# A mixture-of-experts layer stack: first rows loaded first, routed gathers further ahead, more routed weights held

## The chip, the cores and the metric

The kernel runs on one core of a Trainium2 chip. The metric is the device time of one execution in microseconds (us), the median of several runs; less is better. All data is float32.

The engines are named as the profile names them: PE (matrix multiply; PEld is its weight load), DVE (vector), ACT (scalar functions), POOL (here it issues the indirect DMAs: gathers of rows by an index, and adds of rows into memory by an index), and SP (it issues all other DMAs and computes nothing). Each engine takes its instructions in the order in which they were written and waits at each until its semaphores say that it may start.

## The reference, cut to what matters

The input x has 8 sequences of 512 tokens by 256 channels. Four layers follow each other.

```python
# 1 adapter, weights chosen by a language id per sequence
h = relu(x @ W1[id] + b1[id]);  c0 = layernorm(x + h @ W2[id] + b2[id]) * gamma[id] + beta[id]
# 2 experts choose tokens: 8 experts, each takes its 128 best tokens of every sequence
Sm = softmax(c0 @ Wg.T);  G, I = top_k(Sm transposed, 128)
x1 = x;  x1[b, I] += G * (gelu(c0[b, I] @ W1[e] + b1[e]) @ W2[e] + b2[e])
# 3 conditioning: scans over time, gates, a projection and a layernorm  -> c1
# 4 tokens choose experts: 64 experts, 8 per token, at most 128 tokens per expert
w, ids = top_k(softmax(c1 @ router.T), 8);  w = w / sum(w)
y_e = (silu(rows_e @ w_gate[e]) * (rows_e @ w_up[e])) @ w_down[e]
out = x1 + sum over e of w * y_e  +  (silu(c1 @ s_gate) * (c1 @ s_up)) @ s_down
```

The residuals around the layers are kept in memory (x1 in `x1_rows`, the sum in `out` and a second array `odd`).

## The kernel before

**How the order is made.** The kernel is written as steps: each has an engine, an estimated cost, the keys that it reads and writes, the buffers (rings) that it takes, a rank, and optionally `after`, other steps that must have been placed first. `Order.run` plays these steps against a simple clock and calls their functions in the order in which it lets them start; that is the order of instructions on each engine. Its clock knows one DMA rate (0.19 MB per us) and takes, among steps that can start within 0.25 us, the one of lowest rank. The numbers in it thus change the order of instructions and nothing else. What an instruction waits for on the chip follows from the tiles that it reads and writes, and from the reuse of DMA semaphores.

**Start.** `warm` lets PE multiply the identity seven times four times. `adapter(b)` loads the transposed rows of sequence b (`axb`, `load_xb`), its plain rows (`axt`, `load_xt`), and by POOL gathers the two adapter matrices (`row_w1`, `row_w2`). `down` multiplies on PE (L372), `relu` is on ACT, `up` on PE (L392; for sequences 2 to 4 it also adds axt by a multiplication with the identity, L396), the sum and the statistics are on DVE (L401, L423) for sequences 0, 1 and 5 to 7, and on ACT for 2 to 4. `norm` (ACT, L473), a transposition (PE, L266) with a copy by ACT (L281), and `scores` (PE, L489) follow. Sequences 0 and 1 are the first group: `choose(0)` takes their 128 best tokens per expert in 16 rounds on DVE (L523 to L561), and its lists are turned on PE at L574. `choose(1)` does the same for the other six. `w_load` loads the small weights of the later layers; `hb` is half of the biases that it brings in `cb`.

**Experts.** `expert(n)` runs 32 units (4 pairs of sequences by 8 experts): weights `fw1`, `fw2`, gathers `xg` (L629), PE L642, L663, L730, and adds into `x1_rows`. Behind each pair's experts, `conditioning(b)` and `route(g)` run beside the next pair's. The last pair has none beside it: there DVE ranks tokens (L1229) until `last_lists` writes the 64 lists `ix_c1`. The lower half of the last ranking goes to other partitions by a 32 KB DMA, `rsecond` (L1261), and is merged at L1248.

**Routed experts.** Weights come in 32 pairs of 1.18 MB each (`wpair`, L1398), 6 in the ring `wfar`, 6 in the ring `wnear`. The first six are loaded during the tail of the experts, the next six behind sequence 7's conditioning, ahead of `rsecond`, and pair p beyond that into the place of pair p - 12. `routed(e)` has a gather of 128 rows `xe` (POOL, L1421, a ring of 6), transposition and copy, `gate_up` (PE, L1440), `silu`, `mul`, a transposition (L1455), `down` (PE, L1463 and L1464), a copy `xye` (DVE, L1467), and an `add` into memory (POOL, L1470): even experts into `out`, odd ones into `odd`. Two adds into one array follow each other: the second waits until the first has landed. In the order on POOL eight gathers go ahead of the first add, and later one to three gathers stand between two adds into the same array.

**End.** `total(b)` loads odd and out, adds them and stores the sum.

Of the kernel before, what the change touches and what calls it, by code (L numbers as in the profile page):

```python
# [17 lines left out]
P = 128  # L18
# [7 lines left out]
NH = H // P  # L26
PAIR = 2 * 2 * (H // P) * F1 + 3 * H
FAR = 6
NEAR = 6
WARM = 7  # L30
LATE = ()
EPS = 1e-5
NEG = -3.0e38
# [112 lines left out]
def kernel(ctx: ExitStack, tc: tile.TileContext, d: dict, out: bass.AP):  # L146
# [65 lines left out]

        "rlr": 2, "rtk": 1, "rm8": 2, "rev": 1, "rhalf": 1, "rsecond": 1, "rws": 1, "rc1b": 2, "rsl": 1, "rob": 1,

        "wfar": FAR, "wnear": NEAR, "xe": 6, "xhe": 4, "xeT": 3, "xsl": 2, "xheT": 2, "xye": 4, "xob": len(LATE),
    }
    WHERE = {"mm": "ps", "hid": "ps", "res": "ps"}
    WHERE.update({k: "pa" for k in RINGS if k.startswith("a")})
# [32 lines left out]
    def load(size, fn, **k):  # L251
        return order.add("SP", 0.1, fn, size=size, **k)
# [60 lines left out]
    def adapter(b):  # L313
# [39 lines left out]
            t = tile_of(hT, "ahT", [A + 1, S])  # L353
            nc.gpsimd.memset(t[A : A + 1, :], 1.0)

        rows = []
        if b == 0:
            load(512 * KB, load_xb, new=[(xb, "axb")], rank=b)
        rows.append(pool(1.1, row_w1, new=[(w1, "aw1")], rank=rank - 3, lag=2.5))
        rows.append(pool(1.1, row_w2, new=[(w2, "aw2")], rank=rank - 3, lag=2.5))  # L360

        if b:
            load(512 * KB, load_xb, new=[(xb, "axb")], rank=b, after=rows[:1] if b == 1 else first_up)
        load(512 * KB, load_xt, new=[(xt, "axt")], rank=b, after=rows[1:] if early_one else first_up)
        pool(1.0, one, new=[(hT, "ahT")], rank=rank)
        pool(1.1, row_gains, w=[("gains", b)], rank=rank + 2, lag=2.5)

# [7 lines left out]
            nc.scalar.activation(V[hT][:A, :], V["ph", b][:A, :], AF.Relu, bias=V[w2][:A, H : H + 1])  # L375

        s = pe(2.0 * hot, down, r=[w1, xb, w2, hT], new=[(("ph", b), "mm")], rank=rank, after=() if early_one else begun)
        if early_one:
            first_up[:] = [s]
        act(0.7, relu, r=[("ph", b), w2], w=[hT], rank=rank)  # L380

        sums = ("asum", b)
        for g in range(NC // 2):
# [29 lines left out]
                dve(0.75, add, r=[po, xt], w=[xa], rank=rank)  # L413
            else:
                act(1.1, add, r=[po], w=[xa, sums], rank=rank)
        load(512 * KB, keep, r=[xt], w=[("x1", b)], rank=rank + 5)

        mv, sd = ("amv", b), ("asd", b)
        if by_dve:
# [59 lines left out]
            nc.sync.dma_start(out=c0_rows[b].rearrange("(c p) h -> p c h", p=P), in_=V[c0])  # L479

        act(2.4, norm, r=[xa, ("anm", b)], new=[(c0, "ac0")], rank=rank)
        load(512 * KB, store, r=[c0], w=[("c0", b)], rank=rank)
        turned(c0, c0T, "ac0T", None, rank, lambda: gains[:, b, :], [("gains", b)])

        def scores():
# [26 lines left out]
    def choose(g):  # L512
        n = len(groups[g])
        rank = 10 if g == 0 else 60
        lg = lgs[g]
        lgr = lg.rearrange("p q h (b e) -> p (q h b) e", e=E0)
        G, R = NC * n, n * E0
        K = ("choice", g)
        t = {}

        def less():
            t["mx"] = only([P, G], F32, name=f"mx{g}")
            nc.vector.tensor_reduce(t["mx"], lgr, AX.X, ALU.max)  # L523
            nc.vector.tensor_tensor(lgr, lgr, t["mx"].unsqueeze(2).to_broadcast([P, G, E0]), ALU.subtract)

        def exp():
            nc.scalar.activation(lgr, lgr, AF.Exp)

        def share():
            t["sm"] = only([P, G], F32, name=f"sm{g}")  # L530
            nc.vector.tensor_reduce(t["sm"], lgr, AX.X, ALU.add)
            nc.vector.reciprocal(t["sm"], t["sm"])
            nc.vector.tensor_tensor(lgr, lgr, t["sm"].unsqueeze(2).to_broadcast([P, G, E0]), ALU.mult)

        def turn():
            pt = bank(("cpt", g))
            for q in range(NC // 2):
                nc.tensor.transpose(
                    pt[: 2 * R, q * P : (q + 1) * P], lg[:, q].rearrange("p h r -> p (h r)"), ident
                )  # L540

        def keep():
            t["prob"] = only([2 * R, S // 2], F32, name=f"prob{g}")
            t["best"] = only([2 * R, K0], F32, name=f"best{g}")
            t["best_i"] = only([2 * R, K0], U32, name=f"best_i{g}")
            nc.vector.tensor_copy(t["prob"], V["cpt", g][: 2 * R, : S // 2])

        dve(0.8, less, r=[("lg", g, b) for b in groups[g]], w=[K], rank=rank)
        act(0.35, exp, w=[K], rank=rank, table="e")
        dve(0.9, share, w=[K], rank=rank)  # L550
        pe(0.7, turn, r=[K], new=[(("cpt", g), "mm")], rank=rank)
        s = dve(0.5, keep, r=[("cpt", g)], w=[K], rank=rank)
        if g == 0:
            begun.append(s)
        for i in range(K0 // 8):
            def one(i=i):
                prob, best, best_i = (t[k] for k in ("prob", "best", "best_i"))
                o = slice(8 * i, 8 * i + 8)
                nc.vector.max(best[:, o], prob)
                nc.vector.max_index(best_i[:, o], best[:, o], prob)  # L560
                nc.vector.match_replace(prob, best[:, o], prob, -1.0)  # L561

            dve(1.6, one, w=[K], rank=rank)


        def lists_of():
            t["lists"] = [only([2 * R, K0], F32, name=f"best{k}{g}") for k in "fbr"]
            for dst, src in zip(t["lists"], (t["best_i"], t["best_i"][:, ::-1], t["best"][:, ::-1])):
                nc.vector.tensor_copy(dst, src)

        def turn_lists():
            pt = bank(("clt", g))
            for k, src in enumerate((*t["lists"], t["best"])):
                nc.tensor.transpose(pt[:, 2 * R * k : 2 * R * (k + 1)], src, ident[: 2 * R, : 2 * R])  # L574

        def keep_lists():
            gT = r0.tile([P, R], F32, name=f"gT{g}")
            ix = r0.tile([P, R], I32, name=f"ix{g}")
            first_ones = only([P, R], F32, name=f"fo{g}")
            apart = only([P, R], F32, name=f"ap{g}")  # L580
            n1, n2, v2, v1 = (V["clt", g][:, R * k : R * (k + 1)] for k in (0, 3, 5, 6))
            held = only([P, 2, R], F32, name=f"hd{g}")
            nc.vector.tensor_copy(held[:, 0], n1)
            nc.vector.tensor_copy(held[:, 1], v1)
            nc.vector.tensor_tensor(first_ones, held[:, 1], v2, ALU.is_ge)
            nc.vector.tensor_tensor(gT, held[:, 1], v2, ALU.max)
            half = float(S // 2)
            nc.vector.scalar_tensor_tensor(apart, n2, half, held[:, 0], ALU.add, ALU.subtract)
            nc.vector.tensor_tensor(apart, apart, first_ones, ALU.mult)
            nc.vector.scalar_tensor_tensor(ix, n2, half, apart, ALU.add, ALU.subtract)  # L590
            for b in groups[g]:
                o = (b - groups[g][0]) * E0
                lists[b] = ix[:, o : o + E0], gT[:, o : o + E0]

        dve(0.9, lists_of, w=[K], rank=rank)
        pe(0.5, turn_lists, r=[K], new=[(("clt", g), "mm")], rank=rank)
        dve(1.6, keep_lists, r=[("clt", g)], w=[("lists", g)], rank=rank)
# [4 lines left out]
    def expert(n):  # L602
# [16 lines left out]
        def load_3():  # L619
            nc.sync.dma_start(out=tile_of(b2, "fb2", [P, H]), in_=d["fb2"][e : e + 1, :].to_broadcast([P, H]))  # L620

        load(1024 * KB, load_1, new=[(w1, "fw1")], rank=20 + n, after=first_up)
        load(1024 * KB, load_2, new=[(w2, "fw2")], rank=20 + n, after=first_up)
        load(128 * KB, load_3, new=[(b2, "fb2")], rank=20 + n, after=first_up)

        which = 0 if bs[0] in groups[0] else 1
# [133 lines left out]
    def one(name, shape, src, size, rank=30):  # L760
        def fn():
            W[name] = wp.tile(shape, F32, name=name)
            nc.sync.dma_start(out=W[name], in_=src)
        load(size, fn, w=[name], rank=rank)

    def w_load():

# [623 lines left out]
    def pair(p):  # L1391

        q = p - FAR
        ring = "wfar" if q < 0 or q % (FAR + NEAR) >= NEAR else "wnear"

        def fetch():
            t = tile_of(("pair", p), ring, [P, PAIR])
            nc.sync.dma_start(out=t, in_=d["wpair"][p])  # L1398

        load(PAIR * P * 3, fetch, new=[(("pair", p), ring)], rank=400 + 2 * p, after=last_expert if p < FAR else last_tokens)  # L1400

    def hidden_places():

        def fill():
            for k in range(4):
                t = V["he", k] = tile_of(("he", k), "xhe", [P, 2 * P])
                nc.gpsimd.memset(t[:, F1:] if k % 2 == 0 else t[:, : 2 * P - F1], 0.0)

        pool(1.0, fill, w=[("he", k) for k in range(4)], rank=399, after=last_tokens)

    def routed(e):
        rank = 400 + e
# [60 lines left out]
            )  # L1473

        rows = [(k, b) for b in range(B) for k in ("rows", "shares")]
        pool(1.3, gather, r=["slots", *rows], new=[(xe, "xe")], rank=rank, lag=3.0)
        pe(0.35, turn_x, r=[xe], new=[(px, "mm"), (xeT, "xeT")], rank=rank)
        act(0.9, scale, r=[px, "lgb"], w=[xeT], rank=rank)
        pe(1.3, gate_up, r=[xeT, wp_], new=[(pgu, "hid"), (sl, "xsl")], rank=rank)
# [1 line left out]
        dve(0.5, mul, r=[pgu, sl, xe], w=[he], rank=rank)  # L1481
        pe(0.3, turn_h, r=[he], new=[(pt, "mm"), (heT, "xheT")], rank=rank)
        dve(0.45, keep, r=[pt], w=[heT], rank=rank)
        pe(0.9, down, r=[heT, wp_], new=[(po, "res"), (ye, "xye")], rank=rank)
        dve(0.45, out_of, r=[po], w=[ye], rank=rank)
        pool(1.9, add, r=[ye, *(("sum", j, b) for b in range(B))], w=[("chain", j)], rank=rank, lag=3.0)

# [56 lines left out]
    last_lists()  # L1544
    for b in range(B):
        shared(b)
    for p in range(E1 // 2):
        pair(p)
    hidden_places()
    for e in range(E1):  # L1550
        routed(e)
    for b in range(B):
        total(b)
# [76 lines left out]
```

## Time and profile before

| what | value |
|---|---|
| median of 3 runs | 1177.99 us (1172.96 to 1183.5) |
| profiled execution | 1173.81 us, of it span 1172.0 us |
| PE busy, mean granted clock | 1029.4 us (88%), 0.949 |
| DVE, ACT, POOL busy | 685.1, 486.6, 379.7 us |
| DMA | 221.74 MB, mean 189 GB/s |
| start until expert 0's rows are turned (L642) | 0 to 80.1 us |
| experts and conditioning | 80 to 899 us |
| routed experts (first gather to last add) | 899.4 to 1133.8 us |
| end | to 1172 us |

The span runs from the first to the last instruction that the profiler saw on the core; the execution's own time is 1.8 us longer. A busy share is an average over these stages, which have different limits, so the stages are read one by one, and an idle engine matters only where the next work waits for it.

### The profile page before, as it was taken

What the parts mean: (1) busy time and instruction counts of PE and PEld (TensorE: products, weight loads), DVE (VectorE), ACT (ScalarE), POOL (GpSimd) and SP (SyncE); (2) the same over time, 40 slices, a digit from 0 to 9 for tenths busy, and PEclk for the clock granted to TensorE, in tenths of its full rate; (3) what the DMA queues carried; (4) which work ended last, traced back from release to release, by engine and by line L of the source; (5) the groups of instructions that cost most, each with busy time, mean ns of one, the idle gap of its engine ahead of it and who ended that gap; (6) DMA issues with size and microseconds to landing.
All of it is one profiled execution on the core that took longest, in us unless ns stands there. A gap on an engine that the chain in (4) does not pass through costs nothing. (4 is left out here: it accounts for less than half of the span.)

```text
span 1172.0 us, 12980 instructions
## 1 busy us (share of the span) xinstructions
PE 1029.4 (88%) x4317; PEld 758.2 (65%) x4317; DVE 685.1 (58%) x1447; ACT 486.6 (42%) x1012; POOL 379.7 (32%) x305
## 2 busy tenths in 40 slices
PE   7889999999989999989999999999886888678850
PEld 5668888867778776878686877445453555446530
DVE  3543630169983788965798947698766332233323
ACT  2567444443546444536444535423342333223310
POOL 7231333313232213333222212000002676657850
PEclk8779999999999999999999999999997999899985
DMA  8954666767356775456763634932146888795568
GB/s 263 352 166 151 190 191 197 238 204 217 102 169 202 221 239 162 143 145 208 244 209 112 175 93 120 372 108 71 60 162 227 232 241 237 200 270 93 91 132 355
DMA packets 89602, 221.74 MB, mean 189 GB/s; under 512 B 14896, under 2 KB 62488, under 8 KB 77120
## 3 DMA queue, kind: packets, MB, share of 16 engines
q1 hardware_dynamic: 63936, 183.91, 45.0%
q0 software_dynamic: 25600, 37.01, 16.6%
q8 instruction: 34, 0.56, 0.2%
q14 instruction: 32, 0.26, 0.1%
HBM read 177.69 MB, written 47.32 MB: 192 GB/s over the span
## 5 line engine op out<-in xcount | busy, mean ns | idle before, releaser
L663 PE MATMUL hid<-exT,fw 128*128 128x256 f32 x1024 | 231.6, 382 | 3.3 <-ACT hf L673 3.3
L730 PE MATMUL res<-fw,hf 128*128 128x256 f32 x1024 | 233.0, 379 | 0.0
L663 PEld LDWEIGHTS hid<-exT,fw 128*128 128x128 f32 x1024 | 193.8, 191 | 31.7 <-ACT hf L673 4.5
L730 PEld LDWEIGHTS res<-fw,hf 128*128 128x128 f32 x1024 | 191.6, 190 | 25.7 <-issue 1.4
L748 POOL DMA_INDIRECT x_rows<-y,ix x64 | 117.2, 1832 | 235.9 <-ACT y L745 225.2
L629 POOL DMA_INDIRECT xg<-c_rows,ix x64 | 65.8, 1029 | 241.6 <-PE hid L642 201.8
L673 ACT ACTIVATE hf<-hid,fb 128x256 f32<-128x256 f32 x256 | 104.6, 472 | 76.1 <-PE hid L663 76.0
L1005 DVE TENSOR_TENSOR_SCAN t<-alpha,u 128x512 f32<-128x512 f32 x84 | 102.8, 1224 | 2.9
L994 DVE SCALAR_TENSOR_TENSOR u<-gx,blend,mdb 128x512 f32<-128x512 f32 x128 | 95.3, 745 | 1.1
L745 ACT ACTIVATE y<-y,gT 128x256 f32<-128x256 f32 x64 | 32.2, 507 | 143.5 <-DVE y L742 143.5
L1467 DVE COPY xye<-res 128x256 f32<-128x256 f32 x64 | 27.1, 424 | 106.6 <-PE res L1464 97.3
L1421 POOL DMA_INDIRECT xe<-c_rows,ix_c x64 | 63.6, 993 | 55.4 <-DVE ix_c L1308 35.6
L281 ACT ACTIVATE xeT<-mm,lgb 128x128 f32<-128x128 f32 x128 | 50.4, 455 | 48.6 <-PE mm L1430 46.7
L742 DVE TENSOR_TENSOR y<-res,fb 128x256 f32<-128x256 f32 x64 | 26.6, 419 | 73.4 <-PE res L730 73.3
L1443 ACT ACTIVATE xsl<-hid 128x192 f32<-128x192 f32 x64 | 21.2, 331 | 104.3 <-PE hid L1440 104.3
L281 ACT ACTIVATE exT<-hid,gains 128x128 f32<-128x128 f32 x128 | 48.1, 457 | 29.3 <-PE hid L642 29.3
L1007 DVE TENSOR_TENSOR tmp<-tmp,t 128x512 f32<-128x512 f32 x84 | 58.1, 692 | 2.9
L1470 POOL DMA_INDIRECT out_dram<-xye,ix_c x32 | 51.0, 1592 | 25.7 <-DVE xhe L1446 7.6
L1470 POOL DMA_INDIRECT odd<-xye,ix_c x32 | 50.9, 1590 | 23.4 <-issue 8.0
L1440 PE MATMUL hid<-wfar,xeT 128*128 128x384 f32 x144 | 54.7, 505 | 0.0
L1430 PE MATMUL mm<-ident,xe 128*128 128x128 f32 x128 | 25.3, 292 | 32.7 <-DMA xe<-c_rows,ix_c 32.4
L1458 DVE COPY xheT<-mm 128x256 f32<-128x256 f32 x64 | 26.9, 421 | 45.4 <-PE mm L1455 45.4
(210 smaller groups left out, 1613.1 us busy)
## 6 DMA issues: line engine op xcount, KB each, us to landing
fw<-in_fw_dram SPq DMA_DIRECT2D x64, 1024.0 KB
wfar<-in_wpair_dram SPq DMA_DIRECT2D x18, 1152.0 KB
mdb<-md_rows SPq DMA_DIRECT2D x32, 512.0 KB
wnear<-in_wpair_dram SPq DMA_DIRECT2D x14, 1152.0 KB
axb<-in_xT_dram SPq DMA_DIRECT2D x8, 512.0 KB
axt<-in_x_dram SPq DMA_DIRECT2D x8, 512.0 KB
x_rows<-axt SPq DMA_DIRECT2D x8, 512.0 KB
fb<-in_fb_dram SPq DMA_DIRECT2D x32, 128.0 KB
```

Of the source, the lines that this page charges most:

```text
L281: nc.scalar.activation(dst, src, AF.Identity, bias=gain[:, NH + hc : NH + hc + 1], scale=gain[:, hc : hc + 1])
L629: nc.gpsimd.indirect_dma_start(out=tile_of(("xg", u, b), "xg", [P, H]), out_offset=None, in_=c0_rows[b], in_offset=bass.IndirectOffsetOnAx ...
L663: nc.tensor.matmul(t[:, i, :], V[w1][:, hc, f * P : (f + 1) * P], V[exT][:, hc, :], start=hc == 0, stop=hc == NH - 1,)
L673: nc.scalar.activation(t[:, i, :], p[:, i, :], AF.Gelu_apprx_tanh, bias=fb1[:, e, f : f + 1])
L730: nc.tensor.matmul(V[res][:, :H], V[hf][:, i, j * K0 : (j + 1) * K0], V[w2][:, f, :], start=f == 0, stop=f == NF - 1,)
L748: nc.gpsimd.indirect_dma_start(out=x1_rows[b], out_offset=bass.IndirectOffsetOnAxis(ap=lists[b][0][:, e : e + 1], axis=0), in_=V[y], in_of ...
L994: nc.vector.scalar_tensor_tensor(u, V[K["gx"]][:, hc, :], W["blend"][:, hc, k : k + 1], V[mdb][:, k % 2, :], ALU.mult, ALU.mult,)
L1005: nc.vector.tensor_tensor_scan(t, decay(1 + k), u, 0.0, ALU.mult, ALU.add)
L1007: nc.vector.tensor_tensor(whole, whole, t, ALU.add)
L1421: nc.gpsimd.indirect_dma_start(out=tile_of(xe, "xe", [P, H + E1]), out_offset=None, in_=c1_rows, in_offset=bass.IndirectOffsetOnAxis(ap=ix ...
L1440: nc.tensor.matmul(t[:, : 2 * F1], V[xeT][:, hc, :], wgu()[:, hc, :], start=hc == 0, stop=hc == NH - 1)
L1470: nc.gpsimd.indirect_dma_start(out=odd if j else out, out_offset=bass.IndirectOffsetOnAxis(ap=ix_c1[:, e : e + 1], axis=0), in_=V[ye], in_ ...
```

## The change

It does five things. The two loads of the first sequences' rows (axb and axt of 0, then of 1) are issued ahead of all weights, and the small weights of later layers come behind the first experts' weights. A group of warm-up multiplications is left out (`WARM` 6). The ring of gathered rows has 8 places, and gathers have a rank five experts ahead of the adds. `wnear` has 8 places, so 14 pairs are held. A load of a pair beyond these is given `after` the down step of expert 3n + 1 (n counts from the first such pair). Besides, several estimates that the planner uses are changed: sizes of some loads are halved, one round of the choice costs 1.65 for 1.6, the lag of a gather 5 for 3.

```diff
-NEAR = 6
-WARM = 7
+NEAR = 8
+PACE = 30
+WARM = 6
...
-        "wfar": FAR, "wnear": NEAR, "xe": 6, "xhe": 4, "xeT": 3, "xsl": 2, "xheT": 2, "xye": 4, "xob": len(LATE),
+        "wfar": FAR, "wnear": NEAR, "xe": 8, "xhe": 4, "xeT": 3, "xsl": 2, "xheT": 2, "xye": 4, "xob": len(LATE),
...
-        rows = []
-        if b == 0:
-            load(512 * KB, load_xb, new=[(xb, "axb")], rank=b)
-        rows.append(pool(1.1, row_w1, new=[(w1, "aw1")], rank=rank - 3, lag=2.5))
-        rows.append(pool(1.1, row_w2, new=[(w2, "aw2")], rank=rank - 3, lag=2.5))
-
-        if b:
-            load(512 * KB, load_xb, new=[(xb, "axb")], rank=b, after=rows[:1] if b == 1 else first_up)
-        load(512 * KB, load_xt, new=[(xt, "axt")], rank=b, after=rows[1:] if early_one else first_up)
+        pool(1.1, row_w1, new=[(w1, "aw1")], rank=rank - 3, lag=2.5)
+        pool(1.1, row_w2, new=[(w2, "aw2")], rank=rank - 3, lag=2.5)
+        load(256 * KB, load_xb, new=[(xb, "axb")], rank=b, after=() if early_one else first_up)
+        load(256 * KB, load_xt, new=[(xt, "axt")], rank=b + 0.2, after=() if early_one else first_up)
...
-        if early_one:
-            first_up[:] = [s]
+        if b == 0:
+            first_up.append(s)
...
-            dve(1.6, one, w=[K], rank=rank)
+            dve(1.65, one, w=[K], rank=rank)
...
-        load(1024 * KB, load_1, new=[(w1, "fw1")], rank=20 + n, after=first_up)
-        load(1024 * KB, load_2, new=[(w2, "fw2")], rank=20 + n, after=first_up)
+        early_part = 0.5 if n < 2 else 1
+        load(1024 * KB * early_part, load_1, new=[(w1, "fw1")], rank=20 + n, after=first_up)
+        load(1024 * KB * early_part, load_2, new=[(w2, "fw2")], rank=20 + n, after=first_up)
...
-        load(size, fn, w=[name], rank=rank)
+        load(size / 2, fn, w=[name], rank=rank, after=() if rank < 0 else first_up)
...
-        load(PAIR * P * 3, fetch, new=[(("pair", p), ring)], rank=400 + 2 * p, after=last_expert if p < FAR else last_tokens)
+
+        n = p - FAR - NEAR
+        after = last_expert if p < FAR else last_tokens if n < 0 else downs[PACE * n // 10 + 1 :][:1]
+        load(PAIR * P * 3, fetch, new=[(("pair", p), ring)], rank=400 + 2 * p, after=after)
...
-        pool(1.3, gather, r=["slots", *rows], new=[(xe, "xe")], rank=rank, lag=3.0)
+        pool(1.3, gather, r=["slots", *rows], new=[(xe, "xe")], rank=rank - 5, lag=5.0)
...
-        pe(0.9, down, r=[heT, wp_], new=[(po, "res"), (ye, "xye")], rank=rank)
+        downs.append(pe(0.9, down, r=[heT, wp_], new=[(po, "res"), (ye, "xye")], rank=rank))
...
-    for p in range(E1 // 2):
-        pair(p)
     hidden_places()
     for e in range(E1):
+        if e % 2 == 0:
+            pair(e // 2)
         routed(e)
```

In the order that this builds, PE has both early downs ahead of both early ups, and all adapter steps up to sequence 7's up ahead of expert 0's first transposition; before, expert 0 stood among them. DVE takes hb between the copies of the two score tiles. POOL issues ten gathers ahead of the first add, and from the thirteenth expert on one gather and one add in turn. SP has eight pairs ahead of rsecond, then 18 pairs in a row. Between expert 2 and the last gathering of tokens the orders differ in nothing that matters here.

## Prediction

> **What bounds the kernel now.** I read first the table of windows, cut where the kernel changes stage (columns: window, its length, busy time and instructions of PE, PEld, DVE, ACT, POOL, granted clock, DMA share, GB/s).
>
> ```profile
> 10.00:40.00 30.00, 21.37 (x80) 15.23 (x78) 8.17 (x28) 10.47 (x18) 13.18 (x16) 0.69 1.00 359
> 40.00:80.00 40.00, 32.94 (x122) 23.06 (x123) 25.49 (x102) 22.99 (x72) 12.11 (x14) 0.77 0.73 253
> 80.00:150.00 70.00, 68.91 (x362) 59.98 (x361) 35.43 (x122) 43.88 (x89) 20.84 (x18) 0.98 0.54 168
> 872.00:899.00 27.00, 14.18 (x40) 8.16 (x39) 25.05 (x67) 3.53 (x6) 0.00 (x0) 0.80 0.75 289
> 899.00:1053.00 154.00, 122.56 (x494) 82.81 (x494) 45.95 (x122) 46.22 (x124) 101.54 (x80) 0.93 0.83 231
> 1053.00:1134.00 81.00, 67.69 (x282) 45.46 (x282) 27.44 (x73) 25.88 (x69) 63.88 (x48) 0.96 0.54 92
> ```
>
> From 80 to 700 us PE is full (68.91 of 70 us in the third row) and the change moves no instruction there, so a microsecond won before it reaches the end. Before 80 us PE idles 15.7 us of 70 and runs at 0.69 and 0.77 of its clock: a chain of waits sets the pace. From 899 to 1134 PE isn't full either. There POOL is: the page gives 993 ns for a gather (L1421) and 1591 ns for an add (L1470), and nearly every POOL row follows the last by 0.30 us. One expert costs POOL 0.99 + 0.30 + 1.59 + 0.30 = 3.18 us, so 48 instructions in the last row are 63.9 + 48 x 0.30 = 78.3 of 81 us. With weights loading, 80 instructions are 101.5 + 24.0 = 125.5 of 154: 28.5 us stalled. The timeline of POOL shows such a stall:
>
> ```profile
> 1004.14 1.62 POOL L1470 DMA_INDIRECT odd<-xye,ix_c  x1 [0.30 <-DVE xhe L1446]
> 1006.06 0.99 POOL L1421 DMA_INDIRECT xe<-c_rows,ix_c  x1 [0.30 <-issue]
> 1007.35 1.60 POOL L1470 DMA_INDIRECT out_dram<-xye,ix_c  x1 [0.30 <-issue]
> 1011.37 1.58 POOL L1470 DMA_INDIRECT odd<-xye,ix_c  x1 [2.42 <-issue]
> ```
>
> The add at 1011.37 found its data long ready; it waited for the earlier add into the same array, odd, to land. How long an add takes to land is in the view of L1470, with weights loading and then without:
>
> ```profile
> DMA to landing us min/median/max: 3.7/5.6/10.2
> ...
> DMA to landing us min/median/max: 3.6/3.8/4.7
> ```
>
> **Part 1, the start.** The timeline, cut to the links of the chain:
>
> ```profile
> 11.15 0.47 SPq L327 DMA_DIRECT2D axt<-in_x_dram  x1
> ...
> 19.36 1.29 DVE L401 TENSOR_TENSOR axa<-mm,axt 128x512 f32<-128x512 f32 x2 [11.78 <-DMA axt<-in_x_dram]
> ...
> 20.74 3.75 PE L372 MATMUL mm<-axb,aw 128*128 128x512 f32 x4 [5.44 <-DMA gains<-in_cgb_dram,ix_w]
> ...
> 30.91 2.08 ACT L473 ACTIVATE ac<-axa,anm,ars 128x256 f32<-128x256 f32 x4 [0.44 <-DVE anm L436]
> ...
> 39.41 0.22 DVE L523 TENSOR_REDUCE mx<-lg 128x8 f32<-128x64 f32 x1
> ...
> 67.52 0.28 PE L574 MATMUL mm<-ident,bestf 32*128 32x32 f32 x1 [3.87 <-DVE bestb L569]
> ```
>
> Sequence 0's axt is issued behind fifteen other loads (2.1 MB) and lands at 19.3; sequence 1's down (20.74) follows; the two scores are chosen at 39.41 and the lists turned at 67.52. Afterwards SP issues axb, axt of both sequences within about 4.5 us, 2.1 MB, landed by about 11.5 at the 0.30 MB/us that moved here.
>
> They don't then start at 11.5, for here **a rule speaks against the change**. The Trainium skill (DMA: Bandwidth & Descriptors, "Issuing engines are not separate DMA queues") says that transfers of all issuing engines interleave on the same 16 DMA engines: POOL's four row gathers, which the matmuls need as much, are not hurried by moving SP's loads. The trace agrees: the second took 3.2 us to land, the third, issued at 7.45 into heavier SP traffic, 6.3 us (13.7), the fourth 6.6 us (15.3). If the x loads alone decided, down 1 could start near 11.5 and the gain would be 6 us; by the gathers it starts at 13.8. I take the row.
>
> Then, with before's durations: down 1 ends at 15.7 (1.88), up 0, now ordered behind it, 17.7 (1.96), up 1 19.7. DVE: add 0 to 18.5, its statistics 2.2 to 20.6, add 1 and two small steps to 22.3, statistics 1 24.4. ACT: norm 0 to 23.8, the turned copy 1.6 to 26.1, root and scale, so norm 1 at 26.9 against 30.91: **4.0 us**. The links to 67.52 stay the same length: lists turned at 63.5. On the way PE now also does one more down (1.9) and an up with its identity matmuls (3.5) that before came after 67.5: 5.4 us of PE work in what was idle time. Together 9.4. But the changed PE order puts all adapters ahead of expert 0, so no expert matmul fills the gaps while ACT norms and copies: from norm 2 (about 56) ACT needs some 39 us (six norms at 2.1, six copies at 1.6, sequence 4's sums and squares 4.5, the rest 12) until the last copy at 95. PE's own work from the lists to the last score is 42.7 us before (67.5 to 110.2), less 9.6 that now lies earlier or later, so 96.6: the two are close enough to collide. I take off 1.4: **-8 us**; between +1 (gaps eat all) and -13 (no gap, gathers on time).
>
> Other weights now load behind the first expert weights. Only hb on DVE needs one early (cb): 9.2 MB ahead of it at 0.36 MB/us put it near 31, DVE asks at about 34; if cover fails it costs the difference. One warm-up group less saves 1.35 us of PE in front of a gather: 0. New planner costs and sizes cost nothing themselves; what they reorder is counted above.
>
> **Part 2, two more pairs before the routed stage.**
>
> ```profile
> 871.56 2.99 SPq L1398 DMA_DIRECT2D wnear<-in_wpair_dram  x6
> ...
> 894.57 0.49 SPq L1261 DMA_DIRECT2D rsecond<-rhalf  x1
> ...
> 897.61 0.28 DVE L1248 TENSOR_TENSOR list<-list,rsecond 64x128 f32<-64x128 f32 x1
> ...
> 899.42 1.02 POOL L1421 DMA_INDIRECT xe<-c_rows,ix_c  x1 [35.62 <-DVE ix_c L1308]
> ```
>
> The six loads (7.08 MB) run at 0.43 MB/us until 891, then the store to odd, and the queue is empty at 894.57, when rsecond's 32 KB go; the last merge has them by 897.61. Eight loads last 2.36/0.43 = 5.5 us longer, the queue to about 897.2.[...] The row of axt, issued at 11.15 and landed at 19.3 behind 2 MB, says that transfers of one queue wait their turn: rsecond lands near 899.4. I take the row: **+1.8 us** (0 to 4), on everything after it, POOL's first gather included. Two loads fewer in the routed stage pay in part 3.
>
> **Part 3, the routed stage.** The number of POOL instructions stays, so its floor stays: 64 x 3.18 = 203.5 us against 234.4 now (899.4 to 1133.8), 31 us of stall. What changes is the order. Between two adds into the same array stood one, two or three gathers: 5.07, 6.36 or 7.65 us. Afterwards, past a head of ten gathers, always two: 6.36. An add follows the landing by 0.73 us, so landings up to 5.6 us are then free; with one gather only up to 4.3. Laying before's own 64 landing times along both orders gives stalls of 29.6 us (before) and 27.0: the long landings, 8 to 10 us, stall in either. That PE waits 32.4 us for gathers (L1430) is no gain: where POOL is full they can't come sooner.
>
> **The pace isn't there.** `after=downs[...]` only tells the planner when it may write a load down. In the built SP order nothing stands between the routed loads, and each waits only for PE to be done with the pair fourteen earlier and for the eighth DMA before it. So loads still go at one for two experts, as now, where pairs wait for their place:
>
> ```profile
> SPq L1398 <- PE res L1464: 90.8, 14, 12.4
> ```
>
> They end with expert 35 instead of 39; those four stalled little in excess: another -0.3. Sum of part 3: **-3 us**, bounded by +6 (landings half a microsecond longer: 18 us per microsecond, as below) and -27 (no stall).
>
> **Sum.** -8 + 1.8 - 3 = -9.2 us on the profiled execution's own 1173.8 us (span 1172.0): 1164.6. The median shown, 1178.0, lies 4.2 above it and would give 1168.8; I take the middle, 1167.
>
> **Rivals.**
> - *Start swallowed* (0.24): the ACT-paced adapters keep PE waiting and expert 0 is turned at 80, as now. For it: ACT's 39 us. Against: PE saves a real 5.4 us of work. Part 1 is then 0: 1175.
> - *Stalls go* (0.10): steady gathers even out DMA bursts and landings fall under 5.6 us everywhere: -27 for -3, 1143. For it: 3.8 us without loads. Against: one load per two experts as before, 1.18 MB each.
> - *Slower* (0.09): adds land later. Each microsecond of mean landing beyond 5.6 costs half a microsecond for each of 36 loaded experts, 18 us; at 7.0 instead of the measured 5.65 +24: 1191. It outweighs the start from 6.2 on. For it: DMA share already 0.83, tighter gathers. Against: total bytes are unchanged.
> - *Main case* 0.57: 1167, own range 1157 to 1176.
>
> About 1% is what a measurement of this kernel can tell from no change. Faster by over 1% (under 1166): half of the main case, stalls go, a little of the first rival: 0.45. Slower: the third and a stray: 0.10. Same: 0.45. The range 1147 to 1182 leaves out most of the slower case and of the end of the second.
>
> **What would show it.** axa's wait for axt gone; the choice's first reduction at 34 to 37 instead of 39.4; lists turned at 62 to 65; rsecond's merge later against rhalf by 1 to 3 us; waits of L1398's successor still one per two experts, last load after expert 35; landings unchanged in the loaded stretch. Wrong if expert 0 starts no sooner relative to the lists' turn and PE is idle from 65 to 95, or if the routed stage moves by over 8 us.

## The result, and the profile after

The changed kernel takes 1172.3 us (median of 20 runs, 1165.13 to 1180.27) where the kernel before takes 1179.72 (20 runs): ratio **0.9933**, 95% interval 0.9909 to 0.9956, by which it is 7.9 us less (the medians differ by 7.4). Measured once more beside the experiments it was 0.9946 (0.9922 to 0.9970).

The two profiled executions don't show that difference: 1174.22 us after, 1173.81 before. The 20 executions of one kernel lie 13 to 15 us apart, and the first profile of before was among its shortest; a second one, taken later, has 1178.66. So in what follows the times decide how much a kernel gains, and the profiles where. The profiled execution of `g_only` was one of its slow ones, over 1.5% longer than its fastest, and no stage of it is read.

The table of windows of the changed kernel, cut as that of before (columns as there):

```profile
10.00:40.00 30.00, 23.08 (x77) 16.25 (x78) 10.30 (x39) 10.65 (x18) 13.15 (x16) 0.66 0.94 324
40.00:80.00 40.00, 34.22 (x124) 25.40 (x123) 24.24 (x96) 25.15 (x75) 12.04 (x14) 0.76 0.89 304
80.00:150.00 70.00, 69.53 (x344) 57.93 (x344) 39.12 (x141) 37.92 (x79) 19.22 (x17) 0.92 0.43 129
872.00:899.00 27.00, 19.61 (x49) 10.70 (x47) 24.67 (x55) 6.78 (x10) 0.00 (x0) 0.84 0.89 351
899.00:1053.00 154.00, 119.84 (x483) 81.41 (x484) 49.02 (x139) 45.54 (x122) 99.44 (x79) 0.92 0.81 225
1053.00:1134.00 81.00, 67.91 (x296) 46.67 (x294) 29.03 (x76) 27.25 (x72) 64.49 (x49) 1.00 0.53 87
```

The third row is the surprise: PE is as full as before from 80 to 150, but its granted clock is 0.92 instead of 0.98, and 344 of its instructions fit in instead of 362. The timeline has the links of the start. Both downs now run one behind the other from 11.69 on, when the gathered matrix of the first has landed:

```profile
11.69 5.40 PE L368 MATMUL mm<-axb,aw 128*128 128x512 f32 x8 [2.43 <-DMA aw<-in_cw_dram,ix_w]
...
27.49 2.07 ACT L469 ACTIVATE ac<-axa,anm,ars 128x256 f32<-128x256 f32 x4 [0.44 <-DVE anm L432]
...
36.15 0.22 DVE L519 TENSOR_REDUCE mx<-lg 128x8 f32<-128x64 f32 x1
...
66.32 0.21 DVE L565 CAST bestb<-best_i 32x128 f32<-32x128 uint32 x1
...
70.75 0.25 PE L570 MATMUL mm<-ident,bestf 32*128 32x32 f32 x1
```

Norm 1 is 3.4 us earlier than before and the choice 3.3. But the choice ends only 1.0 us earlier (the same cast of the last result is at 67.30 before), and the lists are turned 3.2 us *later*. ACT shows the first loss. Before (sequence 2's root, L458, and its norm; then the end of the choice on DVE):

```profile
54.84 0.30 ACT L458 ACTIVATE asd<-asq,eps 128x4 f32<-128x4 f32 x1
...
56.32 2.07 ACT L473 ACTIVATE ac<-axa,anm,ars 128x256 f32<-128x256 f32 x4
...
67.30 0.21 DVE L569 CAST bestb<-best_i 32x128 f32<-32x128 uint32 x1
```

After (root and norm are the fourth and fifth line, behind them what waits for them on DVE and PE):

```profile
54.91 0.67 ACT L371 ACTIVATE ahT<-mm,aw 64x512 f32<-64x512 f32 x1
57.48 0.68 ACT L371 ACTIVATE ahT<-mm,aw 64x512 f32<-64x512 f32 x1 [1.91 <-DMA aw<-in_cw_dram,ix_w]
58.19 1.28 ACT L454 ACT_TABLE_LOAD   x1
59.48 0.48 ACT L454 ACTIVATE asd<-asq,eps 128x4 f32<-128x4 f32 x2
60.22 4.04 ACT L469 ACTIVATE ac<-axa,anm,ars 128x256 f32<-128x256 f32 x8 [0.26 <-DVE anm L459]
...
59.81 0.18 DVE L458 RECIPROCAL ars<-asd 128x4 f32<-128x4 f32 x1 [3.22 <-ACT asd L454]
...
60.87 2.80 PE L267 MATMUL mm<-ident,ac 128*128 128x128 f32 x8 [4.46 <-ACT ac L469]
```

Sequence 2's squares were done at 51.2, but its root now stands behind sequence 3's squares and two relus, of which one waits 1.91 us for a gathered matrix. Two things hang on it: DVE, in the middle of the choice, waits 3.22 us for the root (1.23 before), and PE is idle for 4.46 us until the norm lets it turn sequence 2. Then the lists, ready at 66.5, wait on PE behind sequence 4's up and sequence 2's scores:

```profile
68.54 0.59 PE L392 MATMUL mm<-axt,ident 128*128 128x256 f32 x2
68.97 1.85 PE L485 MATMUL mm<-fwg,ac0T 128*128 128x8 f32 x16
```

In the routed stage the pace of the loads and the landings are what they were. First the waits of SP (us in total, times, longest: 6.7 us each, one for two experts), then the landings of L1472 with weights loading and without:

```profile
SPq L1395 <- PE res L1466: 86.7, 13, 10.3
```

```profile
DMA to landing us min/median/max: 3.7/5.5/9.0
DMA to landing us min/median/max: 3.6/3.8/3.9
```

The last load goes at 1043.8, beside the end of expert 35 (its result copied at 1044.2). The stage takes 228.7 us (907.0 to 1135.7) instead of 234.3, and rsecond's merge comes 4.9 us behind its issue instead of 3.0.

### The profile page after: what moved, and what is told of

Read it like the earlier page. It is cut to its first block, busy times and chain, and to the rows that moved or that the text cites. A ratio compares the mean times of both kernels' runs of the same rounds, so it can differ in the third digit from the quotient of the medians.

```text
span 1172.3 us, 12994 instructions
## 1 busy us (share of the span) xinstructions
PE 1035.4 (88%) x4309; PEld 763.3 (65%) x4309; DVE 685.1 (58%) x1447; ACT 484.5 (41%) x1010; POOL 380.2 (32%) x305
## 4 chain that ended last, share of the span: by engine, by line
PE 42%; DVE 32%; DMA 14%; issue 6%; POOL 3%; ACT 2%; SPq 0%; POOLq 0%; DVEq 0%; ACTq 0%
PE res L727 10%; PE hid L660 9%; DVE t L1002 9%; DVE u L991 7%; DVE tmp L1004 4%; DMA odd<-xye,ix_c 4%; PE mm L931 3%; DVE tr L1002 3%; DMA out_dram<-xye,ix_c 3%; PE mm L1039 2%; DMA xe<-c_rows,ix_c 2%; PE hid L1442 2%; PE mm L267 2%; DMA rc1b<-c1T_rows 2%; POOL xe L1423 2%
## 5 line engine op out<-in xcount | busy, mean ns | idle before, releaser
L1472 POOL DMA_INDIRECT out_dram<-xye,ix_c x32 | 50.5, 1580 | 22.6 <-DVE xheT L1460 7.5
L1472 POOL DMA_INDIRECT odd<-xye,ix_c x32 | 50.5, 1578 | 21.4 <-DVE xye L1469 9.3
L1442 PE MATMUL hid<-wnear,xeT 128*128 128x384 f32 x128 | 48.8, 505 | 0.0
L1442 PE MATMUL hid<-wfar,xeT 128*128 128x384 f32 x128 | 47.4, 495 | 0.0
```

The source lines that it names most:

```text
L1442: nc.tensor.matmul(t[:, : 2 * F1], V[xeT][:, hc, :], wgu()[:, hc, :], start=hc == 0, stop=hc == NH - 1)
L1472: nc.gpsimd.indirect_dma_start(out=odd if j else out, out_offset=bass.IndirectOffsetOnAxis(ap=ix_c1[:, e : e + 1], axis=0), in_=V[ye], in_ ...
```

## The experiments

All twelve kernels, stage by stage. "Unit 2" is the start of the third expert's multiplications (L663 before), by when both orders have done the same work but for the warm-up group; the routed stage runs from the first gather to the end of the last add.

| kernel | ratio to before (95%) | unit 2 | unit 2 to rsecond | issue to merge | routed |
|---|---|---|---|---|---|
| before, twice | 1 | 130.8, 130.9 | 763.8, 767.1 | 3.0, 3.0 | 234.3, 237.0 |
| after, twice | 0.9933 (0.9909-0.9956), 0.9946 (0.9922-0.9970) | 134.3, 129.7 | 766.0, 769.3 | 4.9, 4.2 | 228.7, 230.7 |
| s_only | 0.9978 (0.9954-1.0002) | 127.2 | 767.3 | 3.0 | 240.7 |
| g_only | 0.9952 (0.9931-0.9973) | | | | |
| n_only | 1.0008 (0.9980-1.0036) | 131.3 | 770.7 | 4.9 | 232.0 |
| sg | 0.9942 (0.9922-0.9963) | 132.7 | 766.1 | 3.0 | 237.1 |
| root_first | 0.9949 (0.9927-0.9971) | 129.2 | 768.4 | 4.6 | 232.6 |
| act_q | 0.9945 (0.9920-0.9971) | 134.9 | 763.1 | 5.6 | 229.3 |
| pace | 0.9969 (0.9947-0.9992) | 124.1 | 769.4 | 5.6 | 235.1 |
| mixed | 0.9947 (0.9917-0.9978) | 126.5 | 766.3 | 4.7 | 229.9 |
| best | 0.9911 (0.9880-0.9941) | 130.3 | 764.9 | 3.0 | 235.2 |
| four | (part left out) | 132.3 | 763.5 | 5.7 | 208.9 |

### The parts alone

**s_only**: before with every hunk of the start, and WARM 6.

> The kernel before with the start alone changed (first rows' loads ahead, small weights behind the first expert weights, six warm-up groups, the start's planner costs). The forecast's step (-8 us) expects 0.993 of before, the lists turned near 63 and expert unit 2 some 6 to 8 us earlier than the 130.8 of before. The profile of the changed kernel says otherwise: choice begun at 36.2 instead of 39.4, lists turned at 70.8 instead of 67.5, unit 2 at 134.3. If that profile is typical, this kernel shows unit 2 3 to 4 us later than before and a ratio of 1.002 to 1.004.

Ratio 0.9978: 2.6 us gained, between 5.4 gained and 0.2 lost. Unit 2 came at 127.2, not at 134: neither of the two expectations, the gain of 6 to 8 us least of all. Its choice and lists have the times of the changed kernel (35.6, 70.6), so what differs between 127 and 134 lies after the lists.

**g_only**: before with

```diff
-"xe": 6,
+"xe": 8,
-pool(1.3, gather, ..., rank=rank, lag=3.0)
+pool(1.3, gather, ..., rank=rank - 5, lag=5.0)
```

> The kernel before with the gathers alone changed (8 places for gathered rows, rank five ahead, lag 5). The forecast: stalls of POOL in the loaded stretch from 28.5 to about 26 us, 0.998 of before. The rival 'stalls go': 0.977. If the changed kernel's profile (routed stage 228.7 us against 234.4) is typical and the gathers cause it: 0.995. The start has before's order: unit 2 at 130.8 and rsecond's merge at 897.6 within what differs from run to run, which this run measures.

0.9952: 5.7 us gained (3.2 to 8.1). That is more than forecast, near the 0.995 that the changed kernel's profile had suggested, and far from "stalls go".

**n_only**: before with

```diff
-NEAR = 6
+NEAR = 8
```

> The kernel before with eight places in wnear alone, so 14 pairs held and no other load paced differently. The forecast: rsecond's merge 1.8 us later against rhalf's end and next to nothing back, 1.001 of before. By the changed kernel's profile (merge 4.7 us later after its start is taken off): merge near 902, ratio 1.003, unless the last loads, now three pairs earlier relative to the experts, save stalls at the end of the loaded stretch.

1.0008: nothing, within 0.28%. The profile shows both sides of it. The merge waits 4.9 us instead of 3.0, and the routed stage is shorter (232.0; 234.3 to 240.7 in the three profiles with the same gathers and twelve pairs). The profiled execution is again one of the shorter ones (1179.2; median 1182.9). The three parts multiply to 0.9978 x 0.9952 x 1.0008 = 0.9938: they add up.

**after_again**: the changed kernel.

> The changed kernel once more, for a second profile and more times. Its twenty times gave 0.9933 of before, yet its profiled execution (1174.2) is no shorter than that of before (1173.8). If the first profile was typical: choice at 36, lists turned at 70.8, unit 2 at 134.3, first routed gather at 907. If the draw of one execution decides: unit 2 near 125 to 128 and the first gather some 5 to 8 us earlier. Ratio 0.991 to 0.996 under either.

Unit 2 came at 129.7 and the first gather at 905.0, between the two expectations, with the lists turned at 70.4, much as in the first profile. So the two differ in what lies between the lists and unit 2.

**before_again**: the kernel before.

> The kernel before, for a second profile. The first was among the shortest of its executions (1173.8, median of all 1180). Stage by stage, if that draw was short in the routed stage: 238 to 241 us there instead of 234.3 (240.7 in the kernel with the start alone changed, whose routed stage is the same). If it was short in the start: unit 2 at 134 or more with a clock below 1.0 between 75 and 95.

Unit 2 came at 130.9 again, the clock as in the first profile; the 4.9 us between the two executions lie 3.3 behind unit 2 and ahead of rsecond and 2.7 in the routed stage (237.0, a little under the expected 238 to 241), less 1.3 at the end. Before and after, each as the mean of its two profiles: start +1.1, middle +2.2, merge +1.5, routed stage 235.7 to 229.7, **-6.0**, end -1.1. In all that is 2.2 us less, not 7.9: the middle, where the orders differ in nothing that matters, and the start scatter by as much as is to be explained. But what the profiles show as gained, they show in the routed stage.

**sg**: start and gathers, wnear at 6.

> Start and gathers changed, wnear left at 6 places. If the parts add up (0.9978 x 0.9952): 0.993, as fast as the whole change, and the two more pairs are worth nothing. If the two more pairs help the new order of gathers (the routed stage took 228.7 and 230.7 us in the changed kernel's two profiles, 241.5 with the gathers alone): 0.995 or more here, with POOL stalled 28 us and not 22, and with rsecond's merge 3.0 us behind its issue, not 4.2 to 4.9.

0.9942 (0.9922 to 0.9963) holds the sum of its parts, 0.9930, and is no slower than the whole change: by time the two more pairs are worth nothing. The profile has the routed stage at 237.1 instead of 229 to 231, with the merge back at 3.0 us. But this execution is one of the longest of its 22 (1179.0; median 1173.3), by about as much as its stage is longer, so that by itself it doesn't show what the missing pairs cost.

### Where the start's gain went

**root_first**: the changed kernel with

```diff
-act(0.35, root_of, r=[("asq", b)], ...)
+roots.append(act(0.35, root_of, r=[("asq", b)], ...))
-act(1.1, add, r=[po], w=[xa, sums], rank=rank)
+act(1.1, add, r=[po], w=[xa, sums], rank=rank, after=roots[:1] if b == 3 else ())
```

> The changed kernel, with sequence 3's first sum on ACT held back until sequence 2's root, so that ACT takes that root before sequence 3's squares and before the relu that waits for gathered matrices. Theory: what the start didn't gain was lost at this root, 59.5 in the changed kernel against 54.8 before. Then norm 2 starts near 54 instead of 60.2, the choice's wait for the root falls from 3.2 to about 1 us, PE's 4.5 us idle ahead of it go, and expert unit 2 comes about 4 us earlier than in the changed kernel at the same clock (127 and less): 0.9965 of the changed kernel, 0.990 of before. Rival: PE, throttled after its early idle stretches, sets the pace whatever ACT does; then unit 2 stays at 127 to 134 and the ratio at 0.994.

The chain did as the theory says; from its timelines of ACT and PE:

```profile
50.43 0.30 ACT L456 ACTIVATE asd<-asq,eps 128x4 f32<-128x4 f32 x1
...
51.34 2.06 ACT L471 ACTIVATE ac<-axa,anm,ars 128x256 f32<-128x256 f32 x4
...
64.68 0.24 PE L572 MATMUL mm<-ident,bestf 32*128 32x32 f32 x1
```

Norm 2 is 8.9 us earlier than in the changed kernel and the lists 6.1. And yet the ratio stays at 0.9949 and unit 2 at 129.2, as the rival in the expectation had it. The edit did more than was meant: the planner now also put expert 0's first transposition ahead of the last adapters, where PE waits for its rows (0.67 us here, 1.47 for the next one):

```profile
72.82 0.33 PE L641 MATMUL hid<-ident,xg 128*128 128x128 f32 x1 [0.67 <-DMA xg<-c_rows,ix]
```

Most of the rest is in the windows (clock: third column from the right). Before:

```profile
70.00:80.00 10.00, 9.95 (x45) 7.20 (x44) 0.48 (x3) 6.19 (x22) 5.76 (x7) 0.88 0.85 277
80.00:90.00 10.00, 10.00 (x51) 8.06 (x50) 3.72 (x12) 8.68 (x20) 5.28 (x6) 1.00 0.37 114
```

The changed kernel:

```profile
70.00:80.00 10.00, 10.00 (x45) 9.20 (x45) 2.38 (x13) 6.05 (x17) 4.83 (x6) 0.55 0.69 225
80.00:90.00 10.00, 10.00 (x38) 6.77 (x38) 4.96 (x17) 4.44 (x8) 1.44 (x2) 0.67 0.09 30
```

s_only, with the same order of PE:

```profile
70.00:80.00 10.00, 9.69 (x60) 7.78 (x59) 4.96 (x21) 7.52 (x19) 6.08 (x8) 1.00 0.77 232
80.00:90.00 10.00, 9.61 (x60) 7.90 (x60) 5.29 (x18) 6.86 (x14) 0.00 (x0) 1.00 0.15 54
```

root_first:

```profile
80.00:90.00 10.00, 10.00 (x36) 7.48 (x35) 3.13 (x12) 3.52 (x8) 0.00 (x0) 0.56 0.15 53
```

At full clock PE gets through 51 instructions in 80 to 90 (before) or 60 (s_only), at 0.56 to 0.67 through 36 to 38; they aren't quite the same ones. The time from 34 us to unit 2 can be split into windows of 1 us. Counted as lost to the clock is PE's busy time, times one minus the granted clock:

| kernel | PE idle, 34 to 62 | PE idle, 62 to unit 2 | lost to the clock, 34 to 62 | lost, 62 to unit 2 | the rest |
|---|---|---|---|---|---|
| before, before_again, n_only | 4.2-4.4 | 5.0 | 5.9 | 4.9-5.2 | 76.7-76.9 |
| s_only, pace | 8.3, 7.8 | 1.1, 0.9 | 4.2 | 4.3, 2.0 | 75.3, 75.2 |
| after_again, sg, four | 7.9-8.7 | 0.6-0.8 | 4.4-4.5 | 7.3, 10.6, 10.3 | 74.4-75.2 |
| after, act_q | 7.7, 8.9 | 0.5 | 4.4, 4.0 | 13.0, 13.3 | 74.7, 74.1 |
| root_first | 5.7 | 3.4 | 3.9 | 8.1 | 74.0 |
| mixed, best | 5.7, 5.6 | 2.3, 2.1 | 5.0, 6.1 | 5.1, 7.1 | 74.5, 75.4 |

The last column is what would be left at full clock: some 1.4 to 2.8 us less in the new start. Idle time hardly shrank in the seven profiles with the changed kernel's order of PE (the second to fourth row), it moved ahead of 62. What scatters is the clock behind 62: 4.9 to 5.2 us in all three profiles with the start as before, 2.0 to 13.3 in those seven. This is nearly the whole difference between unit 2 at 124 and at 135. On average unit 2 starts at 130.7 us in the seven and at 131.0 in the three.

The Trainium skill (TensorE: Matmul & The Clock Gate, "Part 1: The HAM clock gate") has the clock fall to half after an idle window of about 3.4 us and come back after a busy one. The 4.5 us idle ahead of 60.9 and the half clock after it fit. The second fall doesn't: in the changed kernel PE was busy for all of 70 to 80 and got 0.55.

The traces tell more of it. In the thirteen profiles that are read, the granted clock is 0.50 or 1.00 and nothing between, and it changes only on a grid of 3.41 us, whose place in the span is another one in each execution. These are two neighbouring steps of the grid in the changed kernel, then in s_only, with the same order of PE:

```profile
67.60:71.01 3.41, 3.41 (x27) 3.19 (x26) 0.15 (x1) 2.20 (x11) 1.44 (x2) 1.00 0.96 333
71.01:74.43 3.42, 3.42 (x15) 3.09 (x14) 1.22 (x10) 3.03 (x9) 1.54 (x2) 0.50 0.50 152
```

```profile
67.13:70.54 3.41, 3.41 (x25) 3.19 (x23) 0.00 (x0) 2.33 (x11) 1.18 (x2) 1.00 1.09 363
70.54:73.96 3.42, 3.11 (x23) 2.66 (x22) 1.34 (x10) 3.14 (x11) 1.55 (x3) 1.00 0.53 153
```

Both first steps hold the end of sequence 4's up and the sixteen scores of 8 columns each; half clock follows the one, full clock the other, where the grid lies 0.47 us earlier and the program 0.2. From 12 us on there are 161 falls; 143 follow a step in which PE idled for 0.4 to 3.4 us (median 2.3; all of it in 15 of them), and 18 a step with under 0.3 us of idle. In these 18 PE began 20 to 28 matmuls of 1536 to 2168 output columns in all, while 3040 of the 3064 other such steps at full clock have more. So a step needn't be idle throughout for the clock to fall, as the page has it; here the traces decide. It also falls behind busy steps full of short matmuls, and where the grid lies can decide whether it does. Where exactly the limit is, these runs don't show.

**mixed**: the changed kernel with two planner sizes as before, so that PE's order has expert 0 between the adapters.

```diff
-early_part = 0.5 if n < 2 else 1
+early_part = 1
-load(256 * KB, keep, ...)      load(256 * KB, store, ...)
+load(512 * KB, keep, ...)      load(512 * KB, store, ...)
```

> The changed kernel with two of its planner sizes as before (the first experts' weights, and the stores of x1 and c0, counted whole). x's rows are still loaded first, but ACT takes sequence 2's root right behind its squares, and PE has expert 0's multiplications between the adapters again, as before the change. Theory: the start lost its gain to the root's place (about 4 us) and to PE's clock, which fell to half in a stretch of adapters without experts (5 of 7 profiles of that order, none of three with the old one). Then the clock is full from about 75 us on, PE's loss to the clock behind 62 us is 4 to 5 us and not 7 to 13, unit 2 starts at 122 to 126, and the ratio is 0.990 to 0.991. Rival: the clock falls by chance, not by the order; then unit 2 varies from 124 to 132 here too and the ratio stays at 0.994.

Unit 2 at 126.5, and 5.1 us lost to the clock behind 62, as before; but `best`, with the same start, lost 7.1 and had unit 2 at 130.3, and the ratio of `mixed` is 0.9947, not 0.990: the rival's signs, not the theory's. Its windows show a dip here too:

```profile
70.00:80.00 10.00, 9.44 (x41) 6.89 (x39) 3.67 (x13) 4.56 (x11) 4.09 (x5) 0.66 0.77 258
```

That the stretch of adapters alone brings the clock down is not shown: the deep dips (10 us and more) are in four of the seven profiles of that order, each with a fall of the clock at 71.0 to 72.9 behind a busy step, and in none of the six others, but the time didn't follow.

### The lists and the held pairs

**act_q**: the changed kernel with rsecond's last 32 KB from ACT.

```diff
-nc.sync.dma_start(out=tile_of(key, "rsecond", ...), ...)
+nc.scalar.dma_start(out=tile_of(key, "rsecond", ...), ...)   # last group only
```

> The changed kernel, with rsecond's last 32 KB issued from ACT's queue instead of SP's, behind whose eight weight loads they stood. If transfers of one queue wait their turn, they now land in some 2 to 3 us, the merge follows their issue by 3.0 us as before and not by 4.2 to 4.9, worth 1.2 to 1.9 us: 0.9985 of the changed kernel. If the 16 engines are simply full, nothing changes. If ACT, held at that issue until rhalf is ready, keeps back the shared expert's work: slower by up to 2 us.

The timeline of the changed kernel, then of `act_q`:

```profile
900.28 0.48 SPq L1258 DMA_DIRECT2D rsecond<-rhalf  x1
905.19 0.28 DVE L1245 TENSOR_TENSOR list<-list,rsecond 64x128 f32<-64x128 f32 x1 [1.91 <-DMA rsecond<-rhalf]
```

```profile
898.04 0.50 ACTq L1258 DMA_DIRECT2D rsecond<-rhalf  x1
903.60 0.28 DVE L1245 TENSOR_TENSOR list<-list,rsecond 64x128 f32<-64x128 f32 x1 [2.56 <-DMA rsecond<-rhalf]
```

Another engine's queue doesn't hurry the transfer: DVE still waits, 2.56 us; the transfer landed 4.8 us behind its issue. It isn't the place in SP's queue that delays these 32 KB, but the 16 DMA engines, whose share is 0.93 and more from 878 until 900 in this profile.

**best**: `mixed`, with two of the eight loads sent behind rsecond.

```diff
-after = last_expert if p < FAR else last_tokens if n < 0 else ...
+after = last_expert if p < FAR else last_tokens if n < -2 else sent if n < 0 else ...   # sent: rsecond's step
```

> The kernel 'mixed', with the last two of the eight loads into wnear sent behind rsecond's 32 KB instead of ahead. ACT's queue didn't help those 32 KB: issued at 898.0, merged at 903.6, with the DMA engines full until about 901. If full engines are the cause, six loads end about 5.5 us earlier, the merge follows the issue by 3.0 us again (4.2 to 5.6 with eight), and DVE's stall of about 1.2 us at the shared expert in that stretch goes: 1.5 to 3 us, 0.998 of 'mixed'. If only the number of pairs held in the routed stage matters, nothing: the same as 'mixed'.

```profile
895.15 0.48 SPq L1260 DMA_DIRECT2D rsecond<-rhalf  x1
898.18 0.28 DVE L1247 TENSOR_TENSOR list<-list,rsecond 64x128 f32<-64x128 f32 x1
```

The merge is back at 3.0 us and doesn't wait, as in every profile with six loads ahead of it; with eight it took 4.2 to 5.7. So the eight loads are the cause. (The stall of 1.2 us at the shared expert isn't theirs: before_again and sg have it with six loads, act_q and pace lack it with eight.) But the routed stage went from 229.9 to 235.2 us: the two loads now run beside its first gathers and adds. In these two profiles what pays in the stage is not how many pairs are held but how many have landed before it. Its ratio is the best here, 0.9911, but of six runs only, whose median, 1173.0, is that of `mixed`, 1173.2; and its interval overlaps that of the changed kernel. It can't be called faster.

### What stalls POOL

**four**: the changed kernel with adds in turn into four arrays, of which the totals read two: half of the experts' sums are left out.

```diff
-out=odd if j else out, ...     w=[("chain", j)]
+out=(out, odd, spare[0], spare[1])[e % 4], ...     w=[("chain", e % 4)]
```

> The changed kernel with its adds spread over four arrays, so that three others stand between two adds into the same one; the totals still read two, so half of the experts' sums are left out of the output. If POOL's stalls are nothing but adds that wait for the last add into the same array to land, they go (22 to 25 us in the changed kernel), and the routed stage takes POOL's own 203.5 us and a few more: 205 to 210 instead of 229 to 231. If late weights or the DMA engines' load hold the stage, it stays above 220.

Its timeline of POOL at the place shown of before:

```profile
1002.94 1.01 POOL L1424 DMA_INDIRECT xe<-c_rows,ix_c  x1 [0.30 <-issue]
1004.26 1.58 POOL L1473 DMA_INDIRECT odd<-xye,ix_c  x1 [0.30 <-issue]
1006.15 1.02 POOL L1424 DMA_INDIRECT xe<-c_rows,ix_c  x1 [0.30 <-issue]
1007.47 1.58 POOL L1473 DMA_INDIRECT spare<-xye,ix_c  x1 [0.30 <-DVE xhe L1449]
```

No gap but the 0.30 us. The stage takes 208.9 us, POOL's own 203.5 and 5 more: nearly all of the stall was adds waiting for the add before them in the same array, and no late weights stand behind it.

**pace**: the changed kernel with a wait that SP really has, ahead of each of the 18 later loads.

```diff
+nc.sync.dma_start(out=tick[n : n + 1, :], in_=V["xye", 3 * n + 1][:1, :64])
 nc.sync.dma_start(out=t, in_=d["wpair"][p])
```

> The changed kernel with a real pace: ahead of each of the 18 later pair loads SP sends 256 bytes of expert 3n+1's result to memory and so waits for it; one load for three experts then. If each load holds up adds once, wherever it falls, POOL's stalls stay at 21 to 23 us, only spread over 54 experts instead of 36: within 0.3% of the changed kernel. If thinner loads land adds sooner (landings under the 5.6 us that are free): stalls fall to 10 or 15 us, 0.99 of the changed kernel and 0.984 of before.

SP's timeline has a load every 7.6 to 17.3 us, at most one for three experts, the last at 1095:

```profile
931.67 0.24 SPq L1396 DMA_DIRECT2D tick<-xye  x1
932.00 0.34 SPq L1398 DMA_DIRECT2D wfar<-in_wpair_dram  x1
941.97 0.24 SPq L1396 DMA_DIRECT2D tick<-xye  x1
942.30 0.34 SPq L1398 DMA_DIRECT2D wfar<-in_wpair_dram  x1
```

0.9969, if anything slower than the change (0.9933 and 0.9946). Adds whose result was ready waited for landings some 25 us in all, against 23.6 in the changed kernel: in these two profiles **a load costs its stall wherever it falls**, 1.3 to 1.4 us each (by 18 loads). Most of the rest of its longer stage is adds waiting for an expert's result, 4.5 us of it from expert 60 on.

## Why the prediction was right, and which of its steps were not

**The sum.** Forecast -9.2 us, measured -7.9 (5.2 to 10.7 us less); forecast 1167 us, measured 1172.3, inside the range of 1157 to 1176. That the sum is so close is luck: it came out through two wrong terms that offset each other.

**Part 1, the start: -8 forecast, -2.6 measured** (s_only; between 5.4 gained and 0.2 lost). The first links held, the first down waiting for its gathered matrix: norm 1 at 27.5 for 26.9, the choice at 36.2 for 35.4. The step that failed is "the links to 67.52 stay the same length". ACT's order had changed between them, and the prediction read the changed order of PE only. The root of sequence 2 went from 54.8 to 59.5, in spite of the 3.3 us won; the lists then stood behind 4.2 us of other work on PE. So the "5.4 us of PE work in what was idle time" filled hardly any idle time on balance: 9.2 to 9.4 us idle from 34 us to unit 2 before, 8.2 to 9.4 after. The 1.4 us taken off for adapters paced by ACT had the right sign and the wrong cause: PE wasn't waiting from 65 to 95, and from 70 to 90 it ran at 0.55 to 0.67 of its clock. The prediction had read the clock of the start (0.69 and 0.77) and then reckoned with before's durations, as if it stayed. Its 42.7 us for PE "to the last score" also end too soon: the score that ends at 110.1 is the last but one, the last ends at 116.3. root_first doesn't bring the gain back either, but as it moved expert 0 as well, it doesn't show the root alone.

**The rival "start swallowed"** had expert 0 turned at 80 as before. It was turned at 96.6. In size it comes nearer than the main case: 0 for a measured -2.6, and in the mean of the seven profiles unit 2 starts where it does before. Of the two signs that were to prove the main case wrong one came, expert 0 no sooner against the lists' turn (25.8 us behind it, before 12.6); but as the built order has all adapters ahead of expert 0, that sign would have come in any case. The other, PE idle from 65 to 95, did not: it was busy at a lower clock, which none of the cases had.

**Part 2: +1.8 forecast, +1.2 to +1.9 measured** (merge behind issue 4.2 to 4.9 instead of 3.0; up to 5.7 in the other profiles with eight loads). Right in size. The reason given, that transfers of one queue wait their turn, falls with act_q. The rule of the Trainium skill that was weighed in part 1 (DMA: Bandwidth & Descriptors, "Issuing engines are not separate DMA queues") is what holds here too.

**Part 3: -3 forecast, about -6 measured** (the two pairs of profiles). That the stage is shorter is clear: 228.7 to 232.6 us in the five profiles with the new gathers and fourteen pairs landed before it (pace aside), 234.3 to 240.7 in the three with the old gathers and twelve. How it divides is not. The profiles give it to the pairs: with the new gathers 230.2 us in the mean of those five and 235.2 and 237.1 with twelve pairs landed, with the old ones 232.0 and 237.3. That is 5 to 6 us for the two pairs, forecast as "another -0.3", and 1 to 2 us for the gathers, forecast as -2.6. The times say the opposite: -5.7 (3.2 to 8.1 us less) for the gathers, nothing for the pairs. A part of what the pairs win is given back ahead of the stage, in the merge and, in n_only's profile, in the stretch before rsecond; but where g_only gained its 5.7 us no profile shows. The forecast for the gathers came of laying one set of landings along both orders; laid along them, seven sets, those of later profiles too, give from -3.8 to +2.2. And "always two" gathers between adds into one array holds only from the sixteenth add on; ahead of it both orders have one or two. So how the gain divides between gathers and pairs is **left open**, since one profile of a kernel is worth no more than its scatter of several us.

**The pace** was read rightly out of the waits: it isn't there. pace shows that a real one would not have helped. **The biases** for hb landed at 34.5, not 31, and DVE had been waiting since 30.3; it cost nothing, since the scores came at 35.9.

## What to carry to other kernels

An edit of a planner's estimates is an edit of every engine's order: lay the built order of each engine along the chain that is to become shorter, and look on each for an instruction that now stands behind a wait it does not need. An edit made to test one engine's order does the same, as root_first did. Where an engine's clock changes within a stage, compare the stage over several profiles before it is credited with microseconds. Weights loaded beside a chain of dependent adds cost it a stall each here, paced or not, and what is small and urgent is better sent before the DMA engines are filled, from whichever queue.

## What the runs showed of the hardware

PE's granted clock was 0.50 or 1.00, and changed only every 3.41 us on a grid that lies differently in each execution. It fell behind steps with idle time (143 falls), and behind 18 steps without any to speak of, in which PE had begun 1536 to 2168 columns in 20 to 28 short matmuls. One and the same order of instructions lost 2.0 to 13.3 us to the clock between 62 us and unit 2 in seven profiles. A 32 KB transfer took 4.2 to 5.7 us to be of use behind eight loads of 1.18 MB, 3.0 us or less behind six; from ACT's queue it was no faster (5.6) than from SP's.
